# One PSUM ring, one order of folds and several places in layer 1's product sequence changed in a two-layer gated transformer block

## The chip, the core and the metric

The kernel runs on one core of one Trainium2 chip. Time is device microseconds (us) of one execution, taken as the median of several runs. The profiler records a separate execution, and its rows have the times of that one.

A core has five engines with instruction streams of their own: TensorE (PE in the profile, its weight loads PEld), VectorE (DVE), ScalarE (ACT), GpSimd (POOL) and SyncE (SP), which here only issues DMAs. The streams wait for each other by semaphores. Products are written to PSUM, and from there VectorE or ScalarE copies or combines them into SBUF.

## The reference

`x` has 16 blocks of 128 tokens by 512 features; a context of 16 x 128 x 128 goes with it. Four updates follow one another, each with its own layer norm and gate:

```python
x = x + tanh(g_xattn[0]) * L0_xattn(layernorm(x), ctx)
x = x + tanh(g_ffn[0])   * L0_ffn(layernorm(x))
x = x + tanh(g_xattn[1]) * L1_xattn(layernorm(x), ctx)
x = x + tanh(g_ffn[1])   * L1_ffn(layernorm(x))
```

Layer 0's attention has 16 heads, and its query goes through three weights in a row (`Wq`, `w_kc_q`, `W_qr`) before it meets a key of 64 features. Layer 0's ffn is a 512 - 2048 - 512 network with eight low-rank adapters, two of them chosen for every token:

```python
probs = softmax(x @ Wr + br); w, idx = top_k(probs, 2)
base = x @ W1 + b1
a = gelu(base[:, None] + l1)          # l1: adapters' rank-16 products
mix = (a * combine[:, :, None]).sum(1)
out = mix @ W2 + combine.sum(-1) * b2 + l2   # l2: second adapters
```

Layer 1's attention is causal with 16 heads of 32 features; keys and values come from the context (the latents) through one weight. Layer 1's ffn mixes eight low-rank maps by a softmax over eight logits per token:

```python
h = relu(x @ W1 + b1)
alpha = softmax(h @ W2 + b2)                   # the shares
vx = einsum('krd,bsd->bskr', V, x)             # the ranks
out = einsum('bsk,bskd->bsd', alpha, einsum('kdr,bskr->bskd', U, vx))
```

All of it is computed in fp32.

## The kernel before

**Common helpers.** Tokens are worked on in four groups g = 0 to 3 of four blocks b. Every product goes through `matmul` (L165) and most transposes through `transpose` (L170), so the profile shows these lines for nearly all of TensorE's work, and products are told apart by their tiles. Each fp32 product appears as two records. From the ffn on, `matmul`, `transpose` and `send` (L174) pin their instructions: TensorE and SyncE's DMA queue run them in the order in which the program writes them. `send` issues a DMA on SyncE. SyncE works through its issues one after the other, and one that waits for its data holds up those behind it.

**PSUM.** There are three rings of banks (L63 to L69): `mm` with four, `tr` with two, `acc` with two. A product that takes a tile from a ring waits until the tile that lay in that bank has been read. `drain` copies from PSUM; it alternates between VectorE and ScalarE (`evacuate`, L81), but while `near[0]` is set (between a block's scores and its outward product) it uses VectorE alone.

**Start.** Layer 0's three query weights are multiplied together on the chip, for eight pairs of heads. `load_pair` (L455) loads a pair's weights on SyncE's queue: `wcq`, `wqr`, `wq`. `fold_first` (L483) makes `m_ps` (L491), two tiles of six products, one for each head j; each reads its head of `wcq` and both heads of `wqr`. VectorE copies the result to `m`. `fold_second` (L498) makes `f_ps` (L503) from `m` and `wq`, and ScalarE copies it into the folded weight `fq`. In the loop over pairs, `fold_first` of the next pair is written before `fold_second` of the present one. Between them stand the rotated context's transposes (`kvtr`), keys, layer norm (`xtr_a`) and queries.

**Layer 0's ffn.** For each group, `up_pair`, `adapt_pair` and `adapt` make the hidden layer of 2048 features and the adapters. `adapt` gathers the second adapters' ranks in `t2_ps`, two tiles of the `acc` ring. Then `down` (L1105) makes the way back to 512 features from seven products n = 0 to 6 (a scheme with seven half-size products in place of eight); its PSUM tile is `fy_ps`:

```python
y_ps = (acc_tile if n else mm_tile)(f"fy_ps{g}_{n}")
```

Product 0 stands before the last `adapt`. Behind that come `bias_out` and `second_ranks` (L1095), whose two operations at L1100 on VectorE read `t2_ps`. Then come products 1 to 6, with the next group's routing in between: `route_parts` makes `rT_ps` from the transposed tokens `xnT_f`, which arrive by DMA and which GpSimd reads too (L352, tile `T`). In the last group, layer 1 begins there instead: `standard` (normalise), `tokens(0)` (L1203; 16 DMAs by `turn_all`, L1186, which transpose block by block into `xnT_a`), products 1 and 2, four `queries` (`q_ps`), `latents(0)` (L1170), four `keys` (`k_ps`), and products 3 to 6 between the first scores.

**Layer 1.** `latents(g)` transposes four blocks of context (`kv1tr`), drains them to `kv1T` and issues the load of the next group's context. `score(b)` (L1220) makes a block's values `v_ps` and scores `s_ps`; VectorE scales and masks them into four tiles `e` (L1241), reduces them (L185), ScalarE takes the exponential, and VectorE transposes them into `eb` (L1247). `carry(b)` (L1251) moves the blocks of `eb` by ten DMAs, `values(b)` (L1257, `o_ps`) multiplies by the values, `project(b)` (L1270, `y_ps`) goes outward and adds to `x`.

For the ffn, `ffn_normal(g)` normalises a group into `late`, `ffn_tokens(g)` (L1298) transposes it (`xtr_f`, drained to `xf`), `hidden` (L1304) makes `h_ps`, `share_parts` (L1320) makes `lT_ps` from all four `h` and appends g to `pending`. `settle` (L1328) empties `pending` by calling `shares` (L1333): `l_ps`, the softmax over eight logits on VectorE and ScalarE, then four DMAs to DRAM (`shared`) and eight that read it back broadcast into `late`. `ranks` (L1363) makes `vx_ps` and multiplies it by the shares (L1371), `mixture` (L1373) makes `my_ps` and adds to `x` (L180), `store` sends finished blocks out.

**The order of layer 1's main loop** is written out by hand. Step s works on `values` and `project` of block b = s - 2 and on `score` of block s. Other work (queries, hidden, ranks, mixtures) is a list with the earliest step and a cost for each unit; `take` takes from it in order as the allowance permits. A step runs so: `values(b)`, `settle`; at every fourth s `latents`; `take`; at every fourth s `keys`; at b = 4, 8, 12 `ffn_tokens`; `score(s)`; `settle`; `take`; `project(b)`; `settle`; `take`; `carry(s)`; `store`. With V for values, S for score, y for project, h, lT, l, vx and my as named above, TensorE's order is for example in s = 11 and 12: V, h2, v, S, h3, lT, my, y, l, my; then V, kv1tr, vx0, k0 to k3, v, S, y, vx1, vx2.

Of the kernel before, what the change touches and what calls it, by code (L numbers as in the profile page):

```python
# [16 lines left out]
NB = 16  # L17
# [25 lines left out]
def kernel(  # L43
# [314 lines left out]
    with tc.tile_pool(name="a0", bufs=2) as ap, tc.tile_pool(name="a0s", bufs=3) as sp:  # L358
# [93 lines left out]
        with tc.tile_pool(name="fold", bufs=3, side="right") as fp:  # L452
            loaded = []

            def load_pair(p):  # L455
                wq_p = fp.tile([P, 2, D], F32, tag="wq", name=f"wq_{p}")
                wcq_p = fp.tile([P, 2, QC, P], F32, tag="wcq", name=f"wcq_{p}")
                wqr_p = fp.tile([P, 2, QC, R], F32, tag="wqr", name=f"wqr_{p}")
                hs = slice(2 * p, 2 * p + 2)
                nc.sync.dma_start(  # L460
                    out=wcq_p, in_=wcqT[hs].rearrange("h (p c) k -> p h c k", c=QC)
                )
                nc.sync.dma_start(
                    out=wqr_p, in_=wqr[hs].rearrange("h (p c) r -> p h c r", c=QC)
                )
                nc.sync.dma_start(
                    out=wq_p,
                    in_=wq[2 * p * P : (2 * p + 2) * P, :].rearrange("(h p) d -> p h d", p=P),
                )
                loaded.append((wq_p, wcq_p, wqr_p))  # L470

            load_pair(0)
            kv_0 = load_kv(0)
            nc.scalar.dma_start(out=cos_sb, in_=cos_t)
            nc.scalar.dma_start(out=sin_sb, in_=sin_t)
            for n in range(GB):
                nc.scalar.dma_start(out=xs[n], in_=x[place(n)])
            nc.scalar.dma_start(out=wkr_sb, in_=wkr)
            nc.scalar.dma_start(out=gates[:, 0:2], in_=g_x.partition_broadcast(P))
            nc.scalar.dma_start(out=gates[:, 2:4], in_=g_f.partition_broadcast(P))  # L480
            nc.scalar.activation(gates, gates, AF.Tanh)

            def fold_first(p):  # L483


                _, wcq_p, wqr_p = loaded[p]
                m_sb = fp.tile([P, 2, R], F32, tag="m", name=f"m_{p}")
                for j in range(2):
                    m_ps = mm_tile(f"m_ps{p}_{j}")
                    for c in range(QC):  # L490
                        nc.tensor.matmul(  # L491
                            m_ps[:, : 2 * R], wcq_p[:, j, c, :], wqr_p[:, :, c, :],
                            start=(c == 0), stop=(c == QC - 1),
                        )
                    nc.vector.tensor_copy(m_sb[:, j, :], m_ps[:, ts(j, R)])
                return m_sb

            def fold_second(p, m_sb):  # L498
                wq_p = loaded[p][0]
                for j in range(2):  # L500
                    f_ps = mm_tile(f"f_ps{p}_{j}")
                    for c in range(ND):
                        nc.tensor.matmul(  # L503
                            f_ps[:, ts(c, P)], wq_p[:, j, ts(c, P)], m_sb,
                            start=True, stop=True,
                        )
                    nc.scalar.copy(
                        fq[:, :, ts(2 * p + j, R)],
                        f_ps.rearrange("p (c r) -> p c r", r=P)[:, :, ts(j, R)],
                    )  # L510

            for p in range(1, 3):
                load_pair(p)
            m_next = fold_first(0)
            kvr_0 = rope(0, kv_0)
            tr = tr_tile("kvtr_0")
            for i in range(GB):
                nc.tensor.transpose(tr[:, ts(i, P)], kvr_0[:, i, :], ident)
            kvT_0 = ap.tile([P, GT], F32, tag="kvT", name="kvT_0", bufs=1)
            evacuate(kvT_0, tr)  # L520
            for p in range(NPAIR):
                m_now = m_next
                if p + 3 < NPAIR:
                    load_pair(p + 3)
                if p + 4 == NPAIR:
                    for n in range(GB, KEPT):
                        nc.sync.dma_start(out=xs[n], in_=x[place(n)])
                if p + 1 < NPAIR:
                    m_next = fold_first(p + 1)
                fold_second(p, m_now)  # L530
                k_ps = tr_tile(f"k_ps0_{p}")
                key(k_ps, p, kvT_0)
                for v in range(2):
                    evacuate(k_r[v][p], k_ps[:, ts(v, 2 * P)])
                if p == 0:
                    xnT_0 = layernorm_T("a0", 0)
                q_ps = tr_tile(f"q_ps0_{p}")
                query(q_ps, p, xnT_0)
                for v in range(2):
                    evacuate(q_r[v][p], q_ps[:, ts(v, 2 * P)])  # L540
                if p == NPAIR - 2:
                    deviations(2)
                    normalise(2)
                    roped_1 = rope(1, load_kv(1))
# [560 lines left out]
    def down(q, n):  # L1105


        g = q.g
        a = (q.near[:, :, 0], q.s2, q.far[:, :, 0], s3, q.near[:, :, 1], q.far[:, :, 0],
             q.far[:, :, 1])[n]  # L1110
        w = downs[7 * g + n]
        extra = {2: (0, b2_sb[:, lo]), 3: (1, b2_sb[:, hi]), 5: (0, b2_sb[:, hi]),
                 6: (1, b2_d)}.get(n)
        y_ps = (acc_tile if n else mm_tile)(f"fy_ps{g}_{n}")
        for i in range(2):
            dst = y_ps[:, ts(i, half)]
            for c in range(NF // 2):
                matmul(
                    dst, a[:, c, ts(i, P)], w[:, c, :],
                    start=(c == 0), stop=(c == NF // 2 - 1 and extra is None),  # L1120
                )
            if extra is not None:
                t = 2 * extra[0] + i
                matmul(dst, q.t2[:, ts(t, P)], extra[1], start=False, stop=True)
        if n == 2:
            a12 = q.far[:, :, 0]
            nc.gpsimd.tensor_tensor(a12, a12, q.s2, ALU.subtract)
        targets = (
            ((0, lo), (0, hi), (1, lo), (1, hi)), ((0, hi), (1, lo), (1, hi)), ((0, lo),),
            ((1, lo), (1, hi)), ((0, hi), (1, hi)), ((0, hi),), ((1, lo),),  # L1130
        )[n]
        for i in range(2):
            for h, cols in targets:
                t = 2 * h + i
                dst = xt[g * GB + t][:, cols]
                nc.vector.scalar_tensor_tensor(  # L1136
                    dst, y_ps[:, ts(i, half)], q.first[:, t : t + 1], dst,
                    ALU.mult, ALU.add,
                )
        load_down()  # L1140
# [42 lines left out]
        drain(k_c, k_ps)  # L1183
        ks.setdefault(g, []).append(k_c)

    def turn_all(dst, src):  # L1186

        for t in range(NK):
            for k in range(NK):
                send(dst[ts(k, BK), :, ts(t, BK)], src[ts(t, BK), :, ts(k, BK)])  # L1190

    def standard(xb, g, mv, rstd, layer):

# [8 lines left out]

    def tokens(g, xb):  # L1203
        xa[g] = lnp.tile([P, ND, GT], F32, tag="xnT", name=f"xnT_a1_{g}", bufs=1)
        turn_all(xa[g].rearrange("p c (i t) -> p (c i) t", i=GB), xb)

    def queries(g, c):
        q_ps = tr_tile(f"q1_ps{g}_{c}")
# [72 lines left out]


    xf, hs, al, avT, lTs = {}, {}, {}, {}, {}
    pending = []

    def ffn_normal(g):

# [39 lines left out]

    def settle():  # L1328

        while pending:  # L1330
            shares(pending.pop(0))

    def shares(g):  # L1333
        l_ps = acc_tile(f"l1_ps{g}")
# [62 lines left out]
    def hiddens(g):  # L1397
        for c in range(ND):
            yield 16, lambda c=c: hidden(g, c)
        yield 2, lambda: share_parts(g)  # L1400

    def all_ranks(g):
        for c in range(ND):
# [88 lines left out]
    tokens(0, blocks1[0])  # L1492
    for n in range(1, 3):
        down(q, n)
    for c in range(ND):
        queries(0, c)
    latents(0)
    for c in range(ND):
        keys(0, c)
    tokens(1, blocks1[1])  # L1500
# [19 lines left out]
    for s in range(AHEAD, NB + AHEAD):  # L1520
# [2 lines left out]
        values(b)  # L1523
        settle()
        turn = s < NB and s % GB == 0
        if turn:
            latents(s // GB)
        take(s, first)
        if turn:
            for c in range(ND):  # L1530
                keys(s // GB, c)
            owed[0] -= 17
        if b > 0 and b % GB == 0:
            ffn_tokens(b // GB - 1)
            owed[0] -= 12
        if s == 6:
            standard(late[:, 1], 3, mv1, rstd1, "a1")
            tokens(3, late[:, 1])
        if s < NB:
            score(s)  # L1540
            near[0] = True
        settle()
        take(s + 0.5, second)
        near[0] = False
        project(b)
        settle()
        take(s + 0.5, third)
        if s == AHEAD:
            for b1 in range(NB - GB, NB):
# [8 lines left out]
        store(2)  # L1558
    owed[0] = 0
    take(NB + AHEAD, 1000)  # L1560
    ffn_tokens(NG - 1)
    for _, unit in hiddens(NG - 1):
        unit()
    mixture((NG - 2) * GB + 2)
    store(1)
    settle()
    for _, unit in all_ranks(NG - 1):
        unit()
    for g in (NG - 2, NG - 1):
        for _, unit in mixtures(g, 3 * (NG - 1 - g), 4):  # L1570
            unit()
            store(1)
    store(0)
# [71 lines left out]
```

## Time and profile before

| | us |
|---|---|
| three runs, median | 1572.94 (1572.85 to 1573.02) |
| the profiled execution, its own time | 1570.83 |
| span of its records | 1569.0 |
| folds and start, about | 0 to 98 |
| layer 0's attention, about | 100 to 505 |
| layer 0's ffn, about | 505 to 1119 |
| layer 1, with the last ffn products inside, about | 1119 to 1569 |

A row of a timeline reads: start, duration, engine, line, operation, tile written<-tiles read, shape, how many instructions were put together (x), and in brackets how long the engine had stood before the first of them and what ended that. A row of the waits reads: engine, tile and line that waited, what it waited for, then the total, how often, and the longest. A row of the windows lists the window, its length, the busy time of PE, PEld, DVE, ACT and POOL with the number of instructions, and at its end the granted TensorE clock (1.00 is full speed), the busy share of the DMA engines and GB/s.

### The profile page before, as it was taken

What the parts mean: (1) busy time and instruction counts of PE and PEld (TensorE: products, weight loads), DVE (VectorE), ACT (ScalarE), POOL (GpSimd) and SP (SyncE); (2) the same over time, 40 slices, a digit from 0 to 9 for tenths busy, and PEclk for the clock granted to TensorE, in tenths of its full rate; (3) what the DMA queues carried; (4) which work ended last, traced back from release to release, by engine and by line L of the source; (5) the groups of instructions that cost most, each with busy time, mean ns of one, the idle gap of its engine ahead of it and who ended that gap; (6) DMA issues with size and microseconds to landing.
All of it is one profiled execution on the core that took longest, in us unless ns stands there. A gap on an engine that the chain in (4) does not pass through costs nothing.

```text
span 1569.0 us, 19391 instructions
## 1 busy us (share of the span) xinstructions
PE 1511.1 (96%) x6768; PEld 1018.5 (65%) x6768; DVE 835.3 (53%) x1729; ACT 431.0 (27%) x1421; POOL 436.2 (28%) x437
## 2 busy tenths in 40 slices
PE   7999999999999999999999999999899999999999
PEld 5667878877876666866687667766666444444444
DVE  2265554554565555465645556455546675656422
ACT  2262433343230221022201220122024642434210
POOL 2052632642331332123311332143212221212100
PEclk9999999999999999999999999999999999999999
DMA  8435566543447523622254114521444543232212
GB/s 282 125 77 94 141 174 161 114 119 80 94 64 204 173 73 94 159 98 71 58 140 132 71 71 111 150 71 47 125 117 106 80 61 60 31 69 48 53 49 68
DMA packets 371985, 161.39 MB, mean 103 GB/s; under 512 B 299312, under 2 KB 347184, under 8 KB 369712
## 3 DMA queue, kind: packets, MB, share of 16 engines
q1 hardware_dynamic: 370592, 158.44, 40.3%
q10 hardware_dynamic: 1296, 1.71, 0.3%
q8 instruction: 54, 0.88, 0.2%
q14 instruction: 43, 0.35, 0.1%
HBM read 106.35 MB, written 18.09 MB: 79 GB/s over the span
## 4 chain that ended last, share of the span: by engine, by line
PE 86%; DVE 7%; ACT 3%; SPq 1%; DMA 1%; issue 1%; POOL 1%; DVEq 0%; ACTq 0%; POOLq 0%
PE y_ps L165 14%; PE fy_ps L165 13%; PE q_ps L165 9%; PE l_ps L165 7%; PE hs_ps L165 7%; PE t_ps L165 7%; PE ht_ps L165 5%; PE c_ps L165 4%; PE vx_ps L165 3%; PE s_ps L165 3%; PE my_ps L165 3%; PE h_ps L165 3%; PE k_ps L165 3%; ACT e L190 2%; SPq L175 1%
## 5 line engine op out<-in xcount | busy, mean ns | idle before, releaser
L1076 POOL TENSOR_TENSOR near<-base,a 128x512 f32<-128x512 f32 x32 | 41.7, 1303 | 349.5 <-ACT base L1073 208.2
L197 POOL TENSOR_TENSOR e<-e,rden_a 128x512 f32<-128x512 f32 x64 | 66.6, 1041 | 258.6 <-DVE rden_a L195 256.6
L643 POOL TENSOR_TENSOR e<-e,rden_a 128x512 f32<-128x512 f32 x64 | 66.2, 1041 | 189.1 <-DVE rden_a L641 189.1
L165 PE MATMUL l_ps<-t,b_sb 128*128 128x512 f32 x256 | 115.2, 593 | 1.4 <-DVE t L1011 1.4
L165 PE MATMUL q_ps<-xnT_a,fq 128*128 128x256 f32 (+1 forms) x448 | 115.8, 410 | 0.7 <-ACT xnT_a L87 0.7
L1073 ACT ACTIVATE a<-a 128x512 f32<-128x512 f32 x64 | 40.3, 630 | 276.8 <-DVE a L1072 276.8
L636 ACT ACTIVATE e<-s_ps,nmx_a 128x128 f32<-128x128 f32 x256 | 90.7, 386 | 86.1 <-DVE nmx_a L625 38.6
L190 ACT ACTIVATE e<-e,nmx_a 128x128 f32<-128x128 f32 x256 | 98.8, 387 | 34.2 <-DVE nmx_a L185 34.2
L1072 DVE TENSOR_TENSOR a<-l_ps,base 128x512 f32<-128x512 f32 x64 | 44.0, 688 | 110.9 <-PE l_ps L165 110.8
L165 PEld LDWEIGHTS q_ps<-xnT_a,fq 128*128 128x128 f32 x448 | 84.8, 190 | 25.8 <-issue 11.5
L1136 DVE SCALAR_TENSOR_TENSOR x<-fy_ps,gw,x 128x256 f32<-128x256 f32 x112 | 46.4, 476 | 101.6 <-PE fy_ps L165 101.6
L165 PEld LDWEIGHTS l_ps<-t,b_sb 128*128 128x128 f32 x256 | 48.6, 190 | 61.7 <-issue 58.1
L165 PE MATMUL fy_ps<-ring,far 128*128 128x256 f32 x384 | 87.2, 380 | 0.0
L710 DVE SCALAR_TENSOR_TENSOR x<-y_ps,gates,x 128x256 f32<-128x256 f32 x112 | 48.8, 477 | 70.3 <-PE y_ps L165 70.2
L165 PE MATMUL y_ps<-fo_raw,c 128*128 128x256 f32 x384 | 85.7, 380 | 0.0
L165 PEld LDWEIGHTS fy_ps<-ring,far 128*128 128x128 f32 x384 | 72.6, 190 | 12.3 <-issue 2.5
L165 PEld LDWEIGHTS y_ps<-fo_raw,c 128*128 128x128 f32 x384 | 72.4, 190 | 10.1 <-ACT c L87 0.5
L165 PE MATMUL ht_ps<-T,ring 128*128 128x256 f32 x256 | 65.7, 379 | 0.0
L165 PE MATMUL t_ps<-base,a_sb 128*128 128x512 f32 x128 | 65.4, 592 | 0.0
L165 PE MATMUL t_ps<-a,a_sb 128*128 128x512 f32 x128 | 65.4, 592 | 0.0
L165 PEld LDWEIGHTS s_ps<-k,q 32*128 32x128 f32 (+1 forms) x960 | 50.6, 187 | 20.3 <-issue 16.5
L165 PEld LDWEIGHTS hs_ps<-xnT_f,ring 128*128 128x128 f32 x256 | 48.4, 190 | 22.7 <-issue 14.8
(240 smaller groups left out, 2976.4 us busy)
## 6 DMA issues: line engine op xcount, KB each, us to landing
ring<-w SPq DMA_DIRECT2D x32, 896.0 KB, 4.5
eT<-eb SPq DMA_DIRECT2D x336, 64.0 KB, 2.3
ring<-w SPq DMA_DIRECT2D x16, 1024.0 KB, 5.3
ring<-in_f_w SPq DMA_DIRECT2D x12, 1024.0 KB, 6.6
late<-eb SPq DMA_DIRECT2D x80, 64.0 KB, 2.3
wq<-in_wq SPq DMA_DIRECT2D x8, 512.0 KB, 5.3
quarters<-in_f_w SPq DMA_DIRECT2D x32, 128.0 KB, 2.7
w<-sums SPq DMA_DIRECT2D x8, 512.0 KB, 3.4
```

Source lines behind the costliest of these rows:

```text
L165: ins = nc.tensor.matmul(*args, **kw)
L175: ins = nc.sync.dma_start(out=dst, in_=src)
L190: nc.scalar.activation(dst[:, ts(i, P)], src[:, ts(i, P)], AF.Exp, bias=nmx[:, i : i + 1], accum_out=den[:, i : i + 1],)
L197: nc.gpsimd.tensor_tensor(d3, d3, rden.unsqueeze(2).to_broadcast([P, 4, P]), ALU.mult)
L636: nc.scalar.activation(e[:, ts(i, P)], s_ps[:, ts(i, P)], AF.Exp, bias=nmx[:, i : i + 1], accum_out=den[:, i : i + 1],)
L643: nc.gpsimd.tensor_tensor(e3, e3, rden.unsqueeze(2).to_broadcast([P, 4, P]), ALU.mult)
L710: pin(nc.vector.scalar_tensor_tensor(dst, y_ps, gate_x[0], dst, ALU.mult, ALU.add))
L1072: nc.vector.tensor_tensor(a, l_ps, base, ALU.add)
L1073: nc.scalar.activation(a, a, AF.Gelu_apprx_tanh)
L1076: nc.gpsimd.tensor_tensor(mix, base, second, ALU.add)
L1136: nc.vector.scalar_tensor_tensor(dst, y_ps[:, ts(i, half)], q.first[:, t : t + 1], dst, ALU.mult, ALU.add,)
```

## The change

It makes seven edits.

1. `down`: the tile of product 1 comes from the `mm` ring, not from `acc`.
2. Start: the first pair's `wcq` and `wqr` are loaded in halves, by head, in the order wcq 0, wqr 0, wcq 1, wqr 1; and `fold_second(0)` is written before `fold_first(1)`.
3. `turn_all` takes a second issuer: of the 16 DMAs of `tokens(0)`, the eight with odd k are issued by ScalarE.
4. `latents(0)` is written before the queries of group 0; `latents(g)` of the other groups moves from the beginning of step 4g to the end of step 4g - 1, behind `project`.
5. `ffn_tokens(1)` and `(2)` are written behind `score` of their step; `ffn_tokens(0)` stays.
6. `share_parts` is no longer called at its place in the list. The group is put into `owing`, and `settle`, when it has emptied `pending`, calls `share_parts` for it. The shares come with the `settle` after that.
7. At the end one mixture is written before `ffn_tokens(3)`, and those behind it move up by one; after the last ranks there are four instead of five.

TensorE's order in the two steps shown above becomes: V, h2, v, S, h3, my, y, lT, kv1tr, my; then V, l, vx0, k0 to k3, v, S, y, vx1, vx2. In step 10 it is V, my, v, S, the 16 transposes of `ffn_tokens(1)`, h0, y, h1 (before: V, my, the transposes, v, S, h0, y, h1). In s = 15 and 16: V, h3, v, S, my, y, lT, my; then V, l, vx0 to vx2, y, vx3 (before: V, h3, v, S, lT, my, y, l, my; then V, vx0 to vx2, y, vx3).

```diff
+                for j in ((0, 1) if p == 0 else (slice(0, 2),)):
+                    nc.sync.dma_start(out=wcq_p[:, j], in_=wcq_in[:, j])
+                    nc.sync.dma_start(out=wqr_p[:, j], in_=wqr_in[:, j])
...
+                if p == 0:
+                    fold_second(p, m_now)
                 if p + 1 < NPAIR:
                     m_next = fold_first(p + 1)
-                fold_second(p, m_now)
+                if p:
+                    fold_second(p, m_now)
...
-        y_ps = (acc_tile if n else mm_tile)(f"fy_ps{g}_{n}")
+        y_ps = (mm_tile if n < 2 else acc_tile)(f"fy_ps{g}_{n}")
...
-    def turn_all(dst, src):
+    def turn_all(dst, src, second=None):
         for t in range(NK):
             for k in range(NK):
-                send(dst[ts(k, BK), :, ts(t, BK)], src[ts(t, BK), :, ts(k, BK)])
+                (second if second and k % 2 else send)(
+                    dst[ts(k, BK), :, ts(t, BK)], src[ts(t, BK), :, ts(k, BK)]
+                )
+    def send_too(dst, src):
+        nc.scalar.dma_start(out=dst, in_=src)
...
-        turn_all(xa[g].rearrange("p c (i t) -> p (c i) t", i=GB), xb)
+        turn_all(
+            xa[g].rearrange("p c (i t) -> p (c i) t", i=GB), xb,
+            send_too if g == 0 else None,
+        )
...
         while pending:
             shares(pending.pop(0))
+        while owing:
+            share_parts(owing.pop(0))
...
-        yield 2, lambda: share_parts(g)
+        yield 2, lambda: owing.append(g)
...
+    latents(0)
     for c in range(ND):
         queries(0, c)
-    latents(0)
...
-        if turn:
-            latents(s // GB)
         take(s, first)
...
-        if b > 0 and b % GB == 0:
-            ffn_tokens(b // GB - 1)
+        if s == 6:
+            ffn_tokens(0)
             owed[0] -= 12
-        if s == 6:
             standard(late[:, 1], 3, mv1, rstd1, "a1")
             tokens(3, late[:, 1])
         if s < NB:
             score(s)
             near[0] = True
+        if b > GB and b % GB == 0:
+            ffn_tokens(b // GB - 1)
+            owed[0] -= 12
         settle()
         take(s + 0.5, second)
         near[0] = False
         project(b)
         settle()
+        if s + 1 < NB and (s + 1) % GB == 0:
+            latents((s + 1) // GB)
...
     take(NB + AHEAD, 1000)
+    mixture((NG - 2) * GB + 2)
+    store(1)
     ffn_tokens(NG - 1)
     for _, unit in hiddens(NG - 1):
         unit()
-    mixture((NG - 2) * GB + 2)
+    settle()
+    mixture((NG - 2) * GB + 3)
     store(1)
     settle()
     for _, unit in all_ranks(NG - 1):
         unit()
     for g in (NG - 2, NG - 1):
-        for _, unit in mixtures(g, 3 * (NG - 1 - g), 4):
+        for _, unit in mixtures(g, 4 * (NG - 1 - g), 4):
             unit()
             store(1)
     store(0)
```

More of the change, by code (lines that the diff above doesn't have):

```diff
@@ L459, in load_pair @@
                 hs = slice(2 * p, 2 * p + 2)
[L460 to L465, printed above, removed]
+                wcq_in = wcqT[hs].rearrange("h (p c) k -> p h c k", c=QC)
+                wqr_in = wqr[hs].rearrange("h (p c) r -> p h c r", c=QC)
+                for j in ((0, 1) if p == 0 else (slice(0, 2),)):
+                    nc.sync.dma_start(out=wcq_p[:, j], in_=wcq_in[:, j])
+                    nc.sync.dma_start(out=wqr_p[:, j], in_=wqr_in[:, j])
                 nc.sync.dma_start(
@@ L1283 @@
     xf, hs, al, avT, lTs = {}, {}, {}, {}, {}
-    pending = []
+    pending, owing = [], []
     def ffn_normal(g):
```

## The prediction

> **What bounds the kernel now.** I read the page's busy table first, then TensorE's waits with their places, then a timeline of each place that the change touches. The forecast is made against the profiled execution: span 1569.0 us, its own time 1570.83. The runs' median, 1572.94, is 2.11 above that, so a difference of d us gives 1572.94 + d.
>
> ```profile
> PE 1511.1 (96%) x6768; PEld 1018.5 (65%) x6768; DVE 835.3 (53%) x1729; ACT 431.0 (27%) x1421; POOL 436.2 (28%) x437
> ```
>
> TensorE (PE) works 1511.1 of 1569.0 us. Only 58 us of idle time are left for any change that removes no product, and this one removes none. PE's program order is fixed, so a late operand stops everything behind it. What stops it:
>
> ```profile
> PE fy_ps L165 <- DVE t L1100: 12.5, 4, 3.1
> PE m_ps L491 <- DMA wqr<-in_wqr: 10.8, 2, 5.5
> ...
> PE k_ps L165 <- ACT kv1T L87: 2.0, 1, 2.0
> ```
>
> Each row: total us, times, longest. The largest is `down`'s second product (fy_ps, n = 1), four times 3.13. It needs none of L1100's data: `t2_ps` holds both banks of the accumulation ring until VectorE (DVE) has read them, and the product wants one. A stall can also cost TensorE its clock:
>
> ```profile
> 621.00:624.00 3.00, 3.00 (x9) 2.37 (x8) 0.06 (x1) 0.00 (x0) 0.00 (x0) 0.50 0.66 98
> ...
> 954.00:957.00 3.00, 3.00 (x15) 2.64 (x14) 0.28 (x1) 0.00 (x0) 0.00 (x0) 1.00 0.68 98
> ```
>
> These are windows just behind two of the four stalls (third figure from the end: granted clock). At 0.50 this product took 8.86 us, at 1.00 7.17, so a drop costs 1.69. Of the four stalls three dropped the clock. So did stalls of 2.88, 2.66 and 2.02 us (windows at 477, 1437 and 1225, with 0.57, 0.53 and 0.50); 2.56 (my_ps, at 1475) and 1.72 (q_ps, at 1136) did not.
>
> **The change part by part** (us, minus is a gain).
>
> *Ring, groups 0 to 2.* Product 1 starts 3.13 earlier, at full clock. In group 0 it ran from 619.79 to 628.6. Next late is the router:
>
> ```profile
> 625.12 1.26 POOL L352 TENSOR_TENSOR T<-xnT_f 128x512 f32<-128x512 f32 x1 [13.29 <-DMA xnT_f<-xb_f]
> ...
> 628.58 1.06 PE L165 MATMUL rT_ps<-xnT_f,wr_sb 128*32 128x512 f32 x8
> ```
>
> Product 1 would end at 619.79 − 3.13 + 7.17 = 623.8, but rT_ps reads xnT_f, whose last DMA landed where GpSimd's row starts, 625.12. So −3.45, with a new wait of 1.3. Group 1: landing at 792.46 against rT_ps at 795.19, −2.7. Group 2: 958.59 against 960.12, −1.5. Together −7.65; without that bound it would be −14.5.
>
> *Ring and second issuing queue, group 3.* Products 1 and 2 end at 1134.2 − 4.7 = 1129.5; then queries(0) wants the 16 transposing DMAs of tokens(0):
>
> ```profile
> 1122.61 11.81 SPq L175 DMA_DIRECT2D xnT_a<-xb_a  x16
> ...
> 1136.15 13.97 PE L165 MATMUL q_ps<-xnT_a,aqo_sb 128*128 128x512 f32 x32 [1.72 <-DMA xnT_a<-xb_a]
> ```
>
> SyncE issues one per 0.74 us, the last at 1134.4, and q_ps starts 1.7 later. Half of them now go through ScalarE's queue. Here the Trainium skill speaks against the edit: "DMA: Bandwidth & Descriptors", "Issuing engines are not separate DMA queues", says that all DMAs run on the same 16 engines and a second issuer saves only issue time, usually small beside the transfer. By the rule alone nothing is gained, and q_ps stays at 1136.15. But the trace has the DMA engines 0.65 busy in that stretch, so 16 transfers fill them for 11.81 x 0.65 = 7.7 us, and issue was the bound: landing at 1122.6 + 7.7 + 1.7 = 1132.0. ScalarE has no work then, so nothing queues behind its issues. I take the row: q_ps at 1131.9, **−4.3**; ends 0 and −5.5.
>
> *latents(0) ahead of queries(0).* Its four transposes and the wait of 0.88 for their copy (k_ps, 1151.44) lie in the wait for the DMAs or beside q_ps: 0.60 + 0.88, **−1.45**.
>
> *First folds.*
>
> ```profile
> 5.29 2.90 PE L491 MATMUL m_ps<-wqr,wcq 128*128 128x128 f32 x12 [5.29 <-DMA wqr<-in_wqr]
> 13.68 2.90 PE L491 MATMUL m_ps<-wqr,wcq 128*128 128x128 f32 x12 [5.50 <-DMA wqr<-in_wqr]
> ```
>
> Even the first m_ps reads both heads of wqr, so halving the loads frees nothing. f_ps of pair 0 (1.95 at full clock, by its row at 35.51, so 3.9 at the half clock that still holds there; now 3.21, from 17.23) moves into the hole that ends at 13.68. The second pair's m_ps then starts near 16, but f_ps no longer stands behind it. Layer norm's transposes, at 21.13 now, come near 19: **−2.1**, ends −0.5 (two more loads in SyncE's queue ahead of pair 1) and −3.5.
>
> *Shares of group 0.* lT_ps no longer waits 0.95 for h (1291.37), and its lone start moves beside q_ps: **−1.8**.
>
> *Tail.* A mixture now stands ahead of xtr_f, which waited 1.52, and of h_ps, which waited 0.88; lT_ps and l_ps follow as before: **−1.3**.
>
> *latents(1), one step earlier.* The waits of 2.02 and 1.00 beside it vanish but come back: k_2 starts at 1228.94 because the second k waits for DVE, which is behind the softmax transposes. kv_2's load, which waits for these transposes, now stands in SyncE's queue ahead of tokens(2), 16 DMAs that q_ps wants at 1233.55. They start about 2 later: **+1.5**, ends −1.7 (a clock drop of 2.02 avoided) and +2.5.
>
> *ffn_tokens(1) behind score(10).* Its copies must pass the scores' on DVE.
>
> ```profile
> 1355.53 1.72 PE L165 MATMUL s_ps<-k,q 32*128 32x128 f32 x32
> 1357.18 3.70 PE L165 MATMUL h_ps<-xf,mw_sb 128*128 128x512 f32 x8
> ```
>
> score's products move up by the transposes' 3.1, to 1352.3. DVE starts its first e 1.2 later (1356.72 against 1355.53 now); four e at 0.65 and three or four reductions at 0.64 stand in front of the four xf copies (0.69 each, all on DVE while the scores are open, two on ScalarE before). Sum 1.2 + 2.6 + 2.4 + 2.8 = 9.0, so h_ps at 1361.3 against 1357.18: **+4.1**, ends +2 and +5. The same for ffn_tokens(2) behind score(14): h_ps at 1444.7 against 1442.99, **+1.7**. It is less, because the present order has a stall of 2.66 and its drop there.
>
> *shares(1).* Now l_ps comes behind values(10), directly before vx_0, which needs the finished shares:
>
> ```profile
> 1388.41 0.95 PE L165 MATMUL l_ps<-fold_sb,lT 128*128 128x8 f32 x8
> ...
> 1394.44 5.24 SPq L175 DMA_DIRECT2D late<-shared  x8
> 1398.60 0.69 DVE L1371 TENSOR_TENSOR late<-vx_ps,late 128x512 f32<-128x512 f32 x1 [3.15 <-DMA late<-shared]
> ```
>
> From l_ps to the first use 10.2 us, through two rounds of DMAs; now a mixture, values and vx_0 cover it. Afterwards l_ps starts near 1392.8 and DVE uses the shares at 1402.1 to 1403.0. The transpose ring has two banks: vx_0 holds one until then, k_0 takes the other, and k_1 waits, to about 1402.9 against 1399.34 now: **+3.5**, a stall near 5. *shares(2)*: l_ps near 1478.2; carry(15)'s ten DMAs and two stores now precede its own in SyncE's queue. First use 1489 (1484.86 now), vx_2 at 1489.9 against 1487.1: **+3.0**, a stall near 3.5.
>
> *Sum:* gains 7.65 + 4.3 + 1.45 + 2.1 + 1.8 + 1.3 = 18.6; losses 1.5 + 4.1 + 1.7 + 3.5 + 3.0 = 13.8; −4.8.
>
> *Clock.* Four new stalls of 3.5 to 5 us (two of ffn_tokens, two of shares). "TensorE: Matmul & The Clock Gate" says, in its table of pitfalls, to leave no idle gap above about 3 us, since one idle window halves the clock. That speaks against these moves. By the rule all four drop it, 4 x 1.69 = +6.8, and shorter waits cost nothing. The rows are less sharp: one stall of 3.13 kept the clock and one of 2.02 lost it, so by them (three of four) the four cost +5.1. I take the rule here, since these stalls are longer than any of the rows: +6.6, with ends +5.1 and +6.8. Total **+1.8**, 1574.7.
>
> **Rivals.** (1) *Faster:* the shares' round trip and DVE's queue are shorter than I lay them, or the stalls miss the clock's window as that of 953.01 did: −4.8, 1568. For it: 2.56 was harmless once. Against: five of the six stalls from 2.66 to 3.13 us cost the clock. (2) *Slower:* the clock falls after waits that I count as harmless. The change leaves five waits of 1.3 to 2.4 where PE ran on or stood otherwise: rT_ps in groups 0 to 2 (1.3, 2.0, 1.5), q_ps at 1129.5 (2.4), q_ps at 1233.55 (about 2). It decides if the limit lies near 1.5 instead of near 2.6: each then costs 1.69, all five +8.4. With three of them +5.1, 1580. For it: the 2.02 at 1224.77 dropped it. Against: 1.38, 1.72 and 2.56 did not, so the length alone doesn't decide. (3) *The second queue doesn't do what it says:* landing stays at 1136.15, +4.3, 1579; for it the skill's rule, against it the share of 0.65.
>
> **Numbers.** Forecast 0.36, faster rival 0.28, slower rival 0.26, no help from the queue 0.10. A measurement of this kernel can tell 0.2%, 3.1 us. The forecast's own range, 1570 to 1579, gives same 0.25, slower 0.08, faster 0.03; rival 1 is faster; rival 2 slower; rival 3 slower 0.06, same 0.04. Hence 0.31, 0.29, 0.40. The range, 1565 to 1582, takes in rival 1 with the low ends of the fold and the queue.
>
> **What shows it.** fy_ps n = 1 without a wait, rT_ps behind xnT_f by DMA; q_ps at about 1132 on the old scale; h_ps behind score waiting for xf; k_1 and vx_2 waiting for late L1371, and clock 0.50 behind them. It is wrong if vx_2 or k_1 doesn't wait, or if rT_ps starts 7 us early.

## The result and the profile after

The changed kernel takes 1582.74 us (median of 4 runs, 1580.01 to 1585.77), the kernel before beside it 1572.89. The ratio is 1.0063, 95% interval 1.0045 to 1.0081: about 10 us slower, where +1.8 was forecast. The profiled execution took 1582.61, span 1580.8, which is 11.8 more than before.

The busy table and TensorE's waits (us in total, times, longest) of the changed kernel:

```profile
PE 1512.9 (96%) x6768; PEld 1016.9 (64%) x6768; DVE 842.2 (53%) x1732; ACT 429.1 (27%) x1418; POOL 436.8 (28%) x437
```
```profile
PE xtr_f L170 <- DVE xf L1157: 8.0, 4, 3.6
PE q_ps L165 <- DMA xnT_a<-xb_a: 7.2, 1, 7.2
PE m_ps L491 <- DMA x<-in_x: 7.2, 1, 7.2
PE vx_ps L165 <- DVE late L1385: 7.2, 1, 7.2
PE rT_ps L165 <- DMA xnT_f<-xb_f: 5.0, 3, 2.8
```

TensorE is busy 1.8 us longer than before and idle 10.0 us longer. The 12.5 us at fy_ps are gone. In their place stand 5.0 at rT_ps, and three waits that were small or absent before: xtr_f for copies on VectorE, q_ps for tokens(0), vx_ps for the shares.

To see where the time went, the start of the same product is compared in both traces. The differences are shifts (after minus before), and the step from one mark to the next belongs to the stage between them. V(b) is the first product of values of block b. The forecast's column has the forecast's own terms, with its 1.65 per clock drop added to the four stalls.

| stage, up to the mark | before | after | shift | step | forecast |
|---|---|---|---|---|---|
| start: xtr_a of the second group | 95.88 | 93.90 | −2.0 | −2.0 | −2.1 |
| ring, groups 0 to 2: third rT_ps | 960.12 | 949.87 | −10.25 | −8.3 | −7.65 |
| group 3, tokens(0), latents(0): V(0) | 1190.86 | 1182.00 | −8.9 | **+1.4** | −5.75 |
| V(2) | 1221.08 | 1212.60 | −8.5 | +0.4 | 0 |
| latents(1): V(3) | 1240.62 | 1235.14 | −5.5 | **+3.0** | +1.5 |
| shares(0): V(8) | 1346.68 | 1339.25 | −7.4 | −1.9 | −1.8 |
| ffn_tokens(1): V(9) | 1367.68 | 1367.59 | −0.1 | **+7.3** | +5.75 |
| shares(1): V(12) | 1432.96 | 1433.87 | +0.9 | +1.0 | +5.15 |
| ffn_tokens(2): V(13) | 1456.92 | 1462.40 | +5.5 | **+4.6** | +3.35 |
| shares(2): V(15) | 1497.56 | 1510.58 | +13.0 | **+7.5** | +4.65 |
| tail: end of the span | 1569.0 | 1580.8 | +11.8 | −1.2 | −1.3 |

In this trace the early gains and the tail came as forecast. Group 3 gained nothing. Three moves of layer 1 cost more than they were charged (ffn_tokens(1), ffn_tokens(2), shares(2)), and so did latents(1) here; shares(1) cost less.

The forecast's signs for the ring are seen in the timeline of TensorE around group 0's product 1 (start, duration, tile, and in brackets how long it stood and for what):

```profile
614.58 7.07 PE L165 MATMUL fy_ps<-ring,s 128*128 128x256 f32 x32
622.63 1.06 PE L165 MATMUL rT_ps<-xnT_f,wr_sb 128*32 128x512 f32 x8 [0.98 <-DMA xnT_f<-xb_f]
```

No wait stands before fy_ps, it runs at full clock (7.07 instead of 8.86), and rT_ps waits for its DMA.

### The profile page after: what moved, and what is told of

Same layout as the page of the kernel before. It is cut to its first block, busy times and chain, and to the rows that moved or that the text cites. A ratio compares the mean times of both kernels' runs of the same rounds, so it can differ in the third digit from the quotient of the medians.

```text
span 1580.8 us, 19396 instructions
## 1 busy us (share of the span) xinstructions
PE 1512.9 (96%) x6768; PEld 1016.9 (64%) x6768; DVE 842.2 (53%) x1732; ACT 429.1 (27%) x1418; POOL 436.8 (28%) x437
## 4 chain that ended last, share of the span: by engine, by line
PE 83%; DVE 6%; SPq 4%; DMA 2%; ACT 2%; POOL 1%; issue 1%; ACTq 0%; DVEq 0%; POOLq 0%
PE y_ps L165 14%; PE q_ps L165 10%; PE fy_ps L165 10%; PE hs_ps L165 7%; PE l_ps L165 7%; PE t_ps L165 7%; PE ht_ps L165 5%; PE h_ps L165 4%; SPq L175 4%; PE c_ps L165 3%; PE vx_ps L165 3%; PE my_ps L165 3%; PE s_ps L165 3%; PE k_ps L165 3%; ACT e L190 1%
## 5 line engine op out<-in xcount | busy, mean ns | idle before, releaser
L165 PE MATMUL q_ps<-xnT_a,aqo_sb 128*128 128x512 f32 x128 | 60.7, 627 | 9.3 <-DMA xnT_a<-xb_a 7.2
L165 PE MATMUL vx_ps<-xf,mw_sb 128*128 128x512 f32 x128 | 59.7, 618 | 7.2 <-DVE late L1385 7.2
```

What stands on the lines that cost most here:

```text
L165: ins = nc.tensor.matmul(*args, **kw)
```

## The experiments

On the chips that ran these, the kernel before had medians of 1571.77 to 1572.55, but single runs spread from 1568 to 1577. A median of five to eight runs of a variant (tokens first has 22) is therefore good to 2 or 3 us, and a stage is judged by the step between the marks around it, as in the table. These steps are not equally steady. In the traces of variants that leave the stage as the change made it, ffn_tokens(1), ffn_tokens(2), shares(1), shares(2) and the tail each repeat within 0.5 us, with two exceptions that are told below; the step of latents(1) lies anywhere from +1.4 to +3.0. The ratios are taken over the runs and are not quotients of the medians.

**The ring alone.**

```diff
 (kernel before)
-        y_ps = (acc_tile if n else mm_tile)(f"fy_ps{g}_{n}")
+        y_ps = (mm_tile if n < 2 else acc_tile)(f"fy_ps{g}_{n}")
```

> The kernel before with the first edit alone (the tile of down's product 1 from the mm ring). Theory (the changed kernel's trace read as a table of shifts): product 1 never waits in any group, rT_ps comes 8 us earlier over groups 0 to 2; in group 3 the queries still wait for the last DMA of tokens(0), so nothing more is gained there, and that wait grows to about 6.4 us and costs the clock about 1.9: 1572.9 - 8.2 + 1.9 = 1566.6. Rival (gains made in the ffn are lost again further down, because layer 1 is held by DVE and DMAs and not by TensorE): 1571 to 1573.

Measured: 1564.75 against 1571.91, ratio 0.9965 (0.9952 to 0.9978), −7.2. Its shift is −7.6 at the third rT_ps, −4.4 at V(0), since q_ps waits 5.72 for tokens(0) and then runs 16.64 us instead of 13.97. After that the shift stays between −4.3 and −5.5 as far as V(13). Then 2.7 go at one place that no edit touches: my_ps waits 2.56 for VectorE as before, but now takes 6.45 instead of 3.70. But for this clock drop, layer 1 takes over what it is given, and by the median the rival (1571 to 1573) falls.

**One queue for tokens(0); both queues with the loads behind.**

```diff
 (changed kernel, first variant)
-            send_too if g == 0 else None,
+            None,
 (changed kernel, second variant, in down and behind queries(0))
-        load_down()
+        if not (g == NG - 1 and n in (1, 2)):
+            load_down()
...
+    load_down()
+    load_down()
```

> The changed kernel with all 16 DMAs of tokens(0) on SyncE's queue. Theory (the second queue let the two loads of ring<-w, 1 MB each, pass the last transposing DMAs, so it gave back what it saved in issue): the first DMA stays at 1112.35, issue takes 11.7, landing 1.7 later, q_ps at 1125.8 against 1126.76: 1581.8, within the spread of the changed kernel. Rival A (the second queue helps by the 4 us of issue as forecast, and something else delays the queries): q_ps near 1130, 1587. Rival B (the second queue itself is the harm): q_ps at 1122, 1577.

> The changed kernel with both queues, and the two loads of ring<-w that products 1 and 2 of the last group issue written behind queries(0). Theory (those loads take the DMA engines from the last transposing DMAs): issue ends at 1119.8, landing 2 later, q_ps at 1121.8 instead of 1126.76, the wait 2.3 instead of 7.2, and perhaps no clock drop (1.9): 1576 to 1578. Rival (the DMA engines need that long for the 16 transposing DMAs whatever else is in the queue): no change, 1582.7.

Measured: 1583.23 with one queue (ratio 1.0072, 1.0054 to 1.009), 1579.48 with the loads behind (1.0055, 1.0042 to 1.0067), both beside the same 1571.91. The whole times hardly tell them apart; the trace does. First the changed kernel, DMA issues of SyncE's queue, then of ScalarE's (start, time of issue, count), and TensorE:

```profile
1112.35 6.43 SPq L175 DMA_DIRECT2D xnT_a<-xb_a  x8
1119.10 0.74 SPq L175 DMA_DIRECT2D ring<-w  x1
...
1112.48 7.28 ACTq L1198 DMA_DIRECT2D xnT_a<-xb_a  x8
...
1126.76 15.87 PE L165 MATMUL q_ps<-xnT_a,aqo_sb 128*128 128x512 f32 x32 [7.22 <-DMA xnT_a<-xb_a]
```

Then one queue:

```profile
1116.56 10.71 SPq L175 DMA_DIRECT2D xnT_a<-xb_a  x16
1127.37 0.57 SPq L175 DMA_DIRECT2D ring<-w  x1
...
1129.22 16.54 PE L165 MATMUL q_ps<-xnT_a,aqo_sb 128*128 128x512 f32 x32 [5.49 <-DMA xnT_a<-xb_a]
```

And both queues with the loads behind:

```profile
1115.32 6.49 SPq L175 DMA_DIRECT2D xnT_a<-xb_a  x8
...
1122.94 1.00 SPq L175 DMA_DIRECT2D ring<-w  x1
...
1126.03 15.67 PE L165 MATMUL q_ps<-xnT_a,aqo_sb 128*128 128x512 f32 x32 [3.54 <-DMA xnT_a<-xb_a]
```

In the changed kernel the issue of the 16 DMAs ended at 1119.8, 3 to 4 us sooner than one queue could (10.71 to 11.81 for all 16), yet q_ps started only 7 us after that. From the first issue to q_ps it took 14.41 us with both queues (13.92 in the next variant, where this part is the same), 12.66 with one queue (12.46 with the ring alone, 13.54 before), and 10.71 with both queues and the loads behind. On SyncE's queue alone the two loads stood behind all 16; with half of the DMAs moved away they follow after eight, and the last transposing DMAs land later. There the first load is issued at 1119.1, while ScalarE is still issuing (to 1119.8); with the loads behind it is issued at 1122.94, just after the last of the 16 (to 1122.8), and 3.7 us are saved. So it is the loads beside them that delay the last ones. Rival B (the queue itself is the harm) falls, and so does the rival that these DMAs need that long in any case. The expected 9.5 us with the loads behind was 1.2 short of the measured 10.71. The loads still start 3.1 us ahead of q_ps there, so a part of this may be theirs; a later place was not tried.

**The old place of share_parts, groups 0 to 2.**

```diff
 (changed kernel)
-        yield 2, lambda: owing.append(g)
+        yield 2, lambda: (owing.append if g in (NG - 1,) else share_parts)(g)
```

> The changed kernel with share_parts of groups 0 to 2 back at its place in the list (group 3 as in the changed kernel). Theory (the late shares(2) stand behind carry(15) and two stores in SyncE's queue): the stall of 7.2 ahead of the third vx_ps goes with its clock drop, -7.5; the four waits for k's drains, -1.0; lT_ps waits again in group 0, +1.6: 1582.7 - 6.9 = 1575.8. Rival (the stalls come back in the old places, 2.56 at my_ps and 0.95 twice at lT_ps, each with a clock drop): 1580.

Measured: 1577.67 beside 1583.23 for the one-queue variant, ratio to before 1.0032 (1.0014 to 1.0051). Steps: shares(2) −2.1 instead of +7.5, shares(1) +0.6 instead of +1.0, and from V(5) to V(8), where group 0's shares lie, 0.0 instead of −1.6. So the late shares are a gain in group 0, nearly nothing in group 1, and a loss in group 2. Of the 9.6 that come back there, 1.4 are lost one stage earlier: ffn_tokens(2) costs +6.0 instead of +4.6, its transposes waiting 4.97 instead of 3.56. From V(5) to V(15) the gain is 7.0, as expected (6.9). The whole time lies between the theory (1575.8) and the rival (1580) and decides nothing; the steps do: my_ps waits 0.43 in group 2's stage instead of 2.56, and shares(2) takes less than in the kernel before.

**carry(15) behind shares(2).**

```diff
 (changed kernel; the lines of step s = NB stand behind its first settle)
-        if s < NB:
+        if s < NB - 1:
             carry(s)
-        store(2)
+            store(2)
+        elif s > NB - 1:
+            store(2)
...
+        if s == NB:
+            carry(NB - 1)
+            store(2)
```

> The changed kernel with carry(15) and the two stores of step 15 written behind shares(2) in step 16. Theory (SyncE's queue: the DMAs of shares(2) stood 3.5 us behind carry(15) and two stores although rows was ready at 1485.3): shared<-rows starts right behind rows, the wait of vx_ps for late falls from 7.2 to about 3.7: -3.4 to -5 against the changed kernel, 1578 to 1579. Rival (the two rounds of DMAs from rows to late are the wait, whatever is queued): no change, 1582.7.

Measured: 1578.99 (ratio 1.0046, 1.0031 to 1.0061), 3.6 below the two other variants run beside it, 1582.5 and 1582.7. SyncE's queue, then VectorE and TensorE in the changed kernel:

```profile
1480.91 6.65 SPq L175 DMA_DIRECT2D late<-eb  x10
1487.60 1.10 SPq L175 DMA_DIRECT2D out<-x  x2
1488.80 1.78 SPq L175 DMA_DIRECT2D shared<-rows  x4
1491.73 5.24 SPq L175 DMA_DIRECT2D late<-shared  x8
...
1485.08 0.21 DVE L1366 STREAM_TRANSPOSE rows<-al 128x32 f32<-128x32 f32 x1
...
1497.60 6.18 PE L165 MATMUL vx_ps<-xf,mw_sb 128*128 128x512 f32 x8 [7.18 <-DVE late L1385]
```

and in the variant:

```profile
1484.62 1.72 SPq L175 DMA_DIRECT2D shared<-rows  x4
1487.46 5.25 SPq L175 DMA_DIRECT2D late<-shared  x8
...
1492.42 3.70 PE L165 MATMUL vx_ps<-xf,mw_sb 128*128 128x512 f32 x8 [2.70 <-DVE late L1385]
```

In the first, rows is ready at 1485.3, but its DMAs are issued from 1488.8, behind carry(15) (late<-eb) and two stores (out<-x). In the variant nothing stands ahead of them. The wait falls by 4.5 us, and with it goes the clock drop: vx_ps takes 3.70 again. The step of shares(2) is +0.6 instead of +7.5.

**The wait filled with products.**

```diff
 (changed kernel, ahead of the third vx_ps of group 2)
+            spare = mm_tile("spare")
+            for d in range(7):
+                matmul(spare, mw_sb[:, ND + d % ND, ts(c, P)], xf[g][:, d % ND, :],
+                       start=True, stop=True)
```

> The changed kernel with seven products that nobody reads (fp32, 128 x 512, about 6.2 us together) ahead of the third vx_ps of group 2, in the wait for late. Theory (the wait also costs the clock): the third vx_ps starts where it did and takes 3.7 instead of 6.2, -2.5, 1580. Rival (only the wait counts; the long vx_ps has another cause, such as its operands): no change, or up to 1 us later.

```profile
1488.82 6.17 PE L165 MATMUL spare<-xf,mw_sb 128*128 128x512 f32 x14
1495.27 3.70 PE L165 MATMUL vx_ps<-xf,mw_sb 128*128 128x512 f32 x8 [0.28 <-DVE late L1390]
```

The same product, of the same operands, takes 3.70 when TensorE was busy before it, 6.18 when it had stood 7 us. The step of shares(2) is +4.2 instead of +7.5. So 2.5 us of that stall's cost is the clock, and the rival (the long vx_ps has another cause) falls. In the whole time it cannot be seen: 1582.52 (ratio 1.0066, 1.0053 to 1.0079), within the spread of the changed kernel.

**ffn_tokens ahead of score.**

```diff
 (changed kernel)
+        if b > GB and b % GB == 0:
+            ffn_tokens(b // GB - 1)
+            owed[0] -= 12
         if s < NB:
             score(s)
             near[0] = True
-        if b > GB and b % GB == 0:
-            ffn_tokens(b // GB - 1)
-            owed[0] -= 12
```

> The changed kernel with ffn_tokens(1) and (2) written ahead of score again. Theory (behind score the four xf copies wait for DVE's score work, PE stands 5.0 us twice, and h_ps then runs 2.1 to 2.9 us longer at the lower clock): -7.3 and -4.6 by the shifts between values(8) and (9) and between values(12) and (13): 11.9 below the changed kernel, 1571. Rival (the clock is lost in any case, since the present order's stall of 2.66 there lowers it too): only the later starts of h_ps come back, 5.2 + 1.7 = 6.9 below the changed kernel, 1576.

Measured: 1568.09 against 1571.77, ratio 0.9977 (0.9968 to 0.9986): this one edit less makes the changed kernel faster than the kernel before. TensorE in the changed kernel, step 10, and below it VectorE at the first copy:

```profile
1347.17 1.09 PE L170 MATMUL xtr_f<-ident,late 128*128 128x128 f32 x8
1351.63 0.66 PE L170 MATMUL xtr_f<-ident,late 128*128 128x128 f32 x4 [3.36 <-DVE xf L1157]
1353.07 1.11 PE L170 MATMUL xtr_f<-ident,late 128*128 128x128 f32 x4 [0.79 <-DVE xf L1157]
1354.97 5.82 PE L165 MATMUL h_ps<-xf,mw_sb 128*128 128x512 f32 x8 [0.78 <-DVE xf L1157]
...
1350.30 0.68 DVE L185 TENSOR_REDUCE nmx_a<-e 128x4 f32<-128x512 f32 x1
1350.89 0.68 DVE L1157 COPY xf<-xtr_f 128x512 f32<-128x512 f32 x1
```

and its window behind the stall beside that of the variant (clock third from the end), the changed kernel first:

```profile
1355.00:1358.00 3.00, 3.00 (x4) 1.45 (x5) 0.18 (x2) 1.25 (x8) 2.08 (x2) 0.50 0.01 3
```
```profile
1355.00:1358.00 3.00, 3.00 (x20) 1.66 (x15) 2.93 (x5) 0.95 (x1) 0.00 (x0) 1.00 0.00 0
```

The third group of transposes needs one of the ring's two banks, and the first copy starts at 1350.89, behind VectorE's score work, though its transposes began at 1347.17; then h_ps takes 5.82 instead of 3.70. In the variant h_ps follows s_ps at once (1355.53, 3.70). Steps: +0.1 instead of +7.3 and −2.4 instead of +4.6 (shares(2) behind them takes +5.4 instead of +7.5, why wasn't tried). The rival (only 6.9 comes back) falls: 14.2 came back in these two stages.

**The load of the next context behind tokens(2).**

```diff
 (changed kernel)
-        if g + 1 < NG:
+        if g + 1 < NG and g != 1:
             load_latents(g + 1)
...
             tokens(2, late[:, 1])
+            load_latents(2)
```

> The changed kernel with the load of group 2's context issued behind tokens(2) instead of inside latents(1). Theory (the load waits for latents(1)'s transposes and holds tokens(2) in SyncE's queue): tokens(2) starts 1.6 earlier, q_ps's wait of 1.95 nearly goes and with it the lower clock of that q_ps (5.1 instead of 3.7): -2.5 to -3.3, 1579.8. Rival (tokens(2)'s landing is set by the DMA engines, or the late k_ps of that step is the loss): under 1 us.

Measured: 1582.70, ratio 1.0069 (1.0057 to 1.0081), no gain. The trace of the changed kernel and of the variant:

```profile
1212.38 0.37 SPq L175 DMA_DIRECT2D kv<-in_kvc  x1
1212.79 12.11 SPq L175 DMA_DIRECT2D xnT_a<-late  x16
...
1226.68 5.10 PE L165 MATMUL q_ps<-xnT_a,aqo_sb 128*128 128x512 f32 x8 [1.95 <-DMA xnT_a<-late]
```
```profile
1211.85 10.96 SPq L175 DMA_DIRECT2D xnT_a<-late  x16
...
1226.56 5.40 PE L165 MATMUL q_ps<-xnT_a,aqo_sb 128*128 128x512 f32 x8 [1.13 <-DMA xnT_a<-late]
```

Against V(2), tokens(2) does start 1.6 earlier, right behind carry(2), but q_ps comes 14.7 us behind its first issue instead of 13.9, so only 0.8 of its wait goes and the clock stays low. The step is +2.5 instead of +3.0. One trace can't tell more: in six variants that leave latents(1) as the change made it the step is +1.4 to +2.8, and in one queue and with the loads behind q_ps does not wait for these DMAs at all. The expected gain isn't seen, and what holds the step stays open; latents(1) alone in its old place was not run.

**What was worth keeping.** From the changed kernel, with ffn_tokens(1) and (2), latents(1) to (3) and shares(1) and (2) back in their old places, and with the loads behind the queries:

```diff
 (changed kernel; with the edits shown above for ffn_tokens and the loads)
-        yield 2, lambda: owing.append(g)
+        yield 2, lambda: (owing.append if g in (0, NG - 1) else share_parts)(g)
...
+        if turn:
+            latents(s // GB)
         take(s, first)
...
-        if s + 1 < NB and (s + 1) % GB == 0:
-            latents((s + 1) // GB)
```

> The changed kernel with those parts kept whose stage got shorter: the ring, the start, latents(0) ahead of the queries, both queues with the two loads of ring<-w behind the queries, the late shares of groups 0 and 3, the tail. Back in the old place: ffn_tokens(1), (2), latents(1) to (3), shares(1), (2). Theory (each loss belongs to its own stage, so they can be taken off one by one): against the kernel before -1 start, -8 ring, -2.5 group 3, 0 for latents(1), -1.6 shares(0), 0 and 0 for the rest of layer 1, -1.2 tail: 14 below the kernel before run beside it, 1558. Rival (what is gained early is lost later, since DVE and DMAs hold layer 1): 5 to 8 below, 1565.

> kept, with the start of the kernel before (whole loads of the first pair, fold_first(1) ahead of fold_second(0)). Theory (the two more DMAs put the first product 2 us later, and the folds moved into the hole give 0 to 4 back, as the clock happens to be): the same as kept within 1.5, with xtr_a of the second group (about 94 to 98) within 2 of the other. Rival (the start is worth the 2.1 of the forecast): 2 above kept.

> kept, with down's product 3 of the last group written ahead of the queries instead of behind score(0), and its load of ring<-w behind them as well. Theory (the queries' wait for tokens(0), 3.5 with the loads behind, can be filled with work that is due anyway, and then costs no clock): the wait goes, and q_ps runs 14.0 instead of 15.7: 4 to 5 below kept. Rival (score(0) comes 4 later, so carry(0) is late for values(0) and the wait turns up there): the same as kept.

> kept_third with the 16 DMAs of tokens(0) on SyncE's queue alone and the loads of ring<-w at their old place behind them. Theory (with product 3 ahead, TensorE arrives at the queries some 3.9 later, and one queue lands 12.5 after its first issue): a wait of about 1.5 to 2 is left that may keep the clock: 1 to 3 above kept_third. Rival (the second queue still decides, with its clock drop): 4 above.

| variant | median, runs | ratio to before (1572.55) | V(0), shift | V(15), shift |
|---|---|---|---|---|
| kept | 1559.75, 6 | 0.9907 (0.988 to 0.9934) | −15.0 | −18.5 |
| with the start of before | 1560.84, 6 | 0.9927 (0.9908 to 0.9946) | −8.4 | −8.2 |
| with product 3 ahead | 1562.19, 6 | 0.9933 (0.9917 to 0.9948) | −9.7 | −9.4 |
| the same, one queue | 1563.49, 8 | 0.9949 (0.9931 to 0.9967) | −5.3 | −3.3 |

kept is 12.8 us faster than the kernel before by the medians, nearly the 14 expected, and the rival (5 to 8) falls. Its traced execution (1551.09) was its fastest, so the shifts in its row are larger than a typical run's. From V(0) to V(15) no block's step is longer by more than 0.9: with the moves of layer 1 back, their losses are gone.

The start is worth nothing that these runs show (1559.75 and 1560.84). In eleven traces with the new start the first product begins at 7.0 to 8.0 and the second group's xtr_a at 93.3 to 98.0 (mean 95.1); in three with the old start, at 5.3 to 5.6 and 94.8 to 95.9 (mean 95.3). The first product comes some 2 us later with the two more DMAs, and by the second group nothing of the start's gain is left on average.

Product 3 ahead of the queries does remove their wait, and the rival's number came, but not by its mechanism alone. The wait turns up at V(0), for carry(0)'s DMAs. These are issued 17.4 us later than in kept (1172.65 and 1155.26), though score(0) is only 6.3 later and VectorE has the last eb of block 0 ready at 1160.9. With product 3 ahead, SyncE's wait, then GpSimd and TensorE:

```profile
SPq L175 <- POOL eT L1520: 11.7, 1, 11.7
```
```profile
1170.82 1.81 POOL L1520 MEMSET eT<- 128x2048 f32 x1
...
1181.18 1.93 PE L165 MATMUL o_ps<-eT,v 128*32 128x128 f32 x32 [6.73 <-DMA eT<-eb]
```

GpSimd clears the tile that carry(0) writes. In kept it did so at 1153.42, ahead of its work on block 1's scores; here it comes behind that work. In the variant with one queue it is the same (cleared at 1175.18, V(0) waits 7.00). So product 3's place wasn't tested by itself; a variant with the clearing earlier was not run.

## Why the prediction was wrong

The sum was +1.8 and the span grew by 11.8 (by the medians, 9.9). Three kinds of term carry the difference of 10.0.

**Group 3, 7.2 of it.** The step that failed is "issue was the bound: landing at 1122.6 + 7.7 + 1.7 = 1132.0", and before it "so nothing queues behind its issues". It is true of ScalarE, and the issue did end 3 to 4 us sooner. But the forecast did not ask what was queued behind tokens(0) on SyncE's own queue. Two loads came forward and delayed the last transposing DMAs, as the loads behind show. The ring's shift is −10.25, so this term puts q_ps at 1121.7 in the new trace; it came at 1126.76, 5.1 later, and behind the wait of 7.22 the lower clock cost another 1.9. The Trainium skill's rule ("DMA: Bandwidth & Descriptors", "Issuing engines are not separate DMA queues"), that all of them run on the same engines and interleave, was set aside for the busy share of 0.65. By the rule q_ps would have kept its place, 1125.9 in the new trace, which is 0.9 from the measured one. The share wasn't wrong about these 16 alone: with the loads behind two queues took 10.7 us against 12.7 with one, though not the 9.4 that the forecast gave them.

**The clock behind the stalls, 4.2 (1.9 of it in group 3, told already).** Drops were forecast at four stalls with 1.65 each, 6.6. They came at three of these, but dearer (h_ps 2.1 and 2.9, vx_ps 2.5), and also behind the waits of 7.22 (1.9) and, in this trace, 1.95 (1.4): 10.8 together. (k_ps behind latents(1) runs slowly in both kernels, 3.66 and 3.30, and is left out.) The 1.69 had been read from products just behind stalls of 3.13; it was taken for a constant.

**Sizes in layer 1.** ffn_tokens(1): h_ps was late by 5.2 with everything taken out that came before (forecast 4.1); 0.7 of the excess is a new wait of my_ps for o1T, ahead of the scores. ffn_tokens(2): 1.7 by the same reckoning, exactly as forecast. shares(2): carry(15) and two stores ahead of shared<-rows were named as the cause, rightly, but the first use was put at 1489 from carry's present times; the DMAs of carry could not start before the last transpose of eb, 1480.8, and the stall was 7.2, not 3.5. latents(1): +3.0 for +1.5 in this trace, but +1.4 to +2.8 in six others, so this term can't be called wrong.

One loss did not come, 4.2 us the other way with its clock drop: shares(1). It hides part of the misses above, which is luck. The step that failed is "vx_0 holds one until then, k_0 takes the other, and k_1 waits". k_1 did not wait for vx_0's bank, which the prediction itself named as a sign of being wrong:

```profile
1395.70 1.02 PE L165 MATMUL k_ps<-kv1T,akv_sb 128*128 128x512 f32 x2
1397.40 1.12 PE L165 MATMUL k_ps<-kv1T,akv_sb 128*128 128x512 f32 x2 [0.68 <-ACT k L87]
1399.31 1.12 PE L165 MATMUL k_ps<-kv1T,akv_sb 128*128 128x512 f32 x2 [0.78 <-DVE k L85]
```

By what each waits for, all four keys went through the other bank, one by one, each behind the copy of the one before it. There are four such waits of 0.7 to 0.8, the last of them at v_ps, and the clock stayed at 1.00. The first use of the shares came at 1408.85, even later than forecast (1402.1 to 1403.0), and no product stood for it.

What was right: the ring in groups 0 to 2 with rT_ps next late (−8.3 for −7.65), shares(0), the tail. From the first c_ps that waits (near 478) to the third rT_ps, the thirteen traces with the ring gain 5.0 to 9.3 us, 8.0 on average. The −2.0 of the start is luck: on average these runs show no gain there. "Without that bound it would be −14.5" counts a clock drop in group 2 that was not there (7.17 at full clock); it is −12.8, and nothing rests on it.

The second rival, a clock drop behind waits of 1.3 to 2.4, failed at rT_ps: waits of 0.98, 2.83 and 1.23 kept the clock at 1.00. It held at q_ps behind latents(1), in this trace; at q_ps behind tokens(0) the wait was 7.22 and not 2.4. With all five drops it would give 1583, close to what was measured, but for other reasons. The third rival named the right place with too small a price.

## What to carry to other kernels

Before part of a queue's work is given to a second queue, ask what stands behind it on the first: that comes forward too and can delay the transfers one is waiting for. A late operand on an in-order engine can be charged twice, once for the wait and once for the clock behind it (7.18 and 2.5 us at vx_ps). Removing most of the wait gave both back; filling it with products gave back the clock alone, and that didn't show in the whole time. When several moves go in together, compare the starts of the same products in both traces stage by stage: here group 3 and moves of layer 1 spent what the rest had gained, and the kernel without those losses is 12.8 us faster than the one before.

## What the runs showed of the hardware

The length of a stall doesn't decide alone whether the clock falls. Waits of 3.22 (q_ps in kept), 2.83 (rT_ps) and 2.70 (vx_ps with carry behind) kept it at 1.00; 3.54 (q_ps with the loads behind) and 1.95 (q_ps behind latents(1), after two shorter waits) lost it. The plainest case is one product with one wait: my_ps behind VectorE's x (L180) waited 2.55 to 2.56 us and took 3.70 before the change and in kept, 5.19 in the variant with the start of before (clock 0.57) and 6.45 with the ring alone (0.50). A wait of 1.7 ahead of the first k_ps behind latents(1) lost the clock in the changed kernel (3.30, clock 0.65) and kept it with one queue (1.98, 1.00). What decides between them isn't shown. A drop cost 1.3 to 2.9 us at the product behind it.

Stages that no edit touches differ from one execution to the next: from the second group's xtr_a to the first c_ps that waits (near 478) it took 381.4 us in the trace of before and 384.9 in that of kept_third_one. That is as much as most single edits here are worth.
